# Sums in nine of sixteen steps, lent sums banks and LayerNorm rows on VectorE in a six-layer encoder

## Chip, cores and metric

The kernel runs on one core of a Trainium2 chip. The metric is the device time of one execution in microseconds; the median of three runs of the kernel before is 3676.25 us (3672.96 to 3681.62).

## The reference

Four blocks work on x of shape [2, 1024, 128] in float32, each as `x = x + block(layernorm(x))`: a Mamba block, a mixture of eight experts with the two best chosen, a six-layer attention encoder, and a feed-forward block with weights and activations rounded to a four-bit format. The change lies in the encoder. One encoder layer, with 16 heads of 8 elements, 1024 positions and two batches, computes:

```
q, k = h @ Wq.T + bq, h @ Wk.T + bk            # per head: [1024, 8]
A    = sum over heads of softmax(q k' / sqrt(8))
A    = softmax((A + 16 exp(-|i - j| / 16)) / 16)   # a second softmax, over the mean of the heads
h1   = LN2(LN1(h + A @ h))                      # each LN with its own gain and shift
f    = relu(h1 @ W1.T + b1) @ W2.T + b2         # 512 hidden units
h    = LN3(h1 + f)
```

This is read from the kernel as well as from the reference: the kernel sums the heads' probabilities before the second exponential. q and k are split into three bfloat16 parts each, so that the score products run in bfloat16.

## The kernel before, in words

The four blocks run one after another (`mamba`, `moe`, `encoder`, `fp4_ffn`). In the class `Encoder` the order of all instructions on PE, DVE, ACT and POOL is the program's own, written out by hand in `run`; only the queue SP, which issues most DMAs, is ordered by the framework.

The encoder has 6 layers x 2 batches = 12 attentions, which alternate between the batches. One attention is 8 tiles of 128 queries, one tile is 16 steps, one per head, so there are 1536 steps. In step s:

- `scores` (L986) issues four score products into a tile `sc` of 128x1024 float32 (L1003), then DVE's negated row maximum (L1010). `sc` has three buffers (`pss`, L692), taken in turn with tag "sc".
- `exponentials` of step s-2 (L1013) lets ACT write `e`, 128x1024, with the row sums z. Every fourth time `scaled` (L1025) takes the reciprocals of z on DVE and multiplies four `e` by them on POOL (L1033).
- The sums over heads (`added`, L1060; `offset` for the distance term, L1052) lag by 8 steps and more. Each is 16 transposing products of PE (L1042) that add into two half-size PSUM tiles, `acc0` and `acc1` (128x512 each, `psa`, L693), which I call the sums banks. The table SUMS (L668) says which heads are added in which of the 16 lagged steps: from step 2 to 15.
- After the last head `second` (L1065) takes the second exponential of the sums on ACT (L1070, `prT`); `mixed` (L1075) multiplies it with h on PE (L1080, `sa`: eight products of 128x129), and `residual` (L1089) divides and adds h on DVE (L1094, L1095).

With p = s mod 16, the sums of a tile stand at p = 10 to 15 and 0 to 7, `second` at p = 7, `mixed` at 9, `residual` at 10.

Between two attentions of a batch comes `between` (L923), once for each half of the batch (four tiles): LN1, LN2, a transposition (`transposed`, L772), four products with W1 ("f1", L942), the products with W2 for four row tiles ("f2", L957), LN3, and `project` (L834): a transposition, the products for q and k ("bq", "bk", L853), their three bfloat16 parts on POOL (L870), stores of these to DRAM, and loads of the next q and k (`load_queries`, L895; `load_keys`, L907). q tiles have three buffers, k tiles five, `e` tiles twelve. A norm (L784) takes statistics on DVE, a logarithm and an exponential on ACT, seven small operations on POOL, four row operations on ACT (L818), and gain and shift on POOL (L828, L830).

These pieces are generators. One piece (in every fourth step two) is advanced per step by `advance_one` (L1137); a yielded number makes a piece wait so many steps, and HOLD marks a product whose result is copied out in the next step by `release`. Every product of these pieces, and `sa`, takes one of the three score buffers through `psum` (L730).

Of the kernel before, what the change touches and what calls it, by code (L numbers as in the profile page):

```python
# [18 lines left out]
P = 128  # L19
# [597 lines left out]

def load_encoder(c, wp, w):

    nc = c.nc  # L620
    t = {}
    for k, n in (("b1", NL * FF // P), ("bq", NL), ("bk", NL)):
        t[k] = wp.tile([n, P], F32, name=f"e_{k}n")
        nc.gpsimd.dma_start(t[k], w[k].rearrange("l (c p) -> (l c) p", p=P))
    return t
# [7 lines left out]
HOLD = "hold"  # L633


class Encoder:
# [30 lines left out]

    SUMS = [  # L668
        (), (), (0,), (1,), (2,), (3,), (4,), (5, 6), (7,), (8,), (9,), (10,), (11, 12), (13,),
        (14,), (15,),  # L670
    ]
    QS = (slice(0, P // 2), slice(P // 2, P))
    BEHIND = 2
    TH = TB // 2
    HL = L // 2

    def __init__(self, c, ctx, x, w, t):
        self.c, self.nc, self.tc = c, c.nc, c.tc
        self.x, self.w, self.t = x, w, t
        nc, tc = self.nc, self.tc  # L680
        pool = lambda name, bufs, **kw: ctx.enter_context(tc.tile_pool(name=name, bufs=bufs, **kw))
        self.wp = pool("c_w", 1)
        self.wl = pool("c_wl", 2)
        self.small = pool("c_small", 3)
        self.act = pool("c_act", 2)
        self.parts = pool("c_parts", 1)
        self.ep = pool("c_e", 12)
        self.kp = pool("c_k", 5)
        self.qp = pool("c_q", 3)
        self.loop = pool("c_loop", 2)  # L690
        self.dram = pool("c_dram", 2, space=bass.MemoryType.DRAM)
        self.pss = pool("c_pss", 3, space=PSUM)  # L692
        self.psa = pool("c_psa", 1, space=PSUM)  # L693
        self.scale = float(DH) ** -0.5
        wp = self.wp

        nrel = 2 * L - P
        self.rel = wp.tile([P, nrel], F32, name="rel")
        nc.gpsimd.iota(
            self.rel,  # L700
            pattern=[[-1, nrel]],
            base=L - P,
            channel_multiplier=1,
            allow_small_or_imprecise_dtypes=True,
        )
        nc.scalar.activation(self.rel, self.rel, AF.Abs, bias=c.zero)
        nc.scalar.activation(self.rel, self.rel, AF.Exp, bias=c.zero, scale=-1.0 / DECAY)
        nc.gpsimd.tensor_scalar(self.rel, self.rel, float(NH), 0.0, ALU.mult, ALU.add)

        self.cols = {}  # L710
        for k in ("b1", "bq", "bk"):
            n = t[k].shape[0]
            src = t[k]
            if k != "b1":
                src = wp.tile([n, DH, NH], F32, name=f"e_{k}o")
                nc.gpsimd.tensor_copy(src, t[k].rearrange("l (h d) -> l d h", d=DH))
                src = src.rearrange("l d h -> l (d h)")
            ps = self.psum(f"ps_e_{k}")
            nc.tensor.transpose(ps[:, :n], src, c.ident[:n, :n])
            self.cols[k] = wp.tile([P, n], F32, name=f"e_{k}")  # L720
            nc.scalar.mul(self.cols[k], ps[:, :n], self.scale if k == "bq" else 1.0)
        self.eps = wp.tile([P, 1], F32, name="eps")
        nc.gpsimd.memset(self.eps, EPS)
        self.weights = {}
        self.h = [None] * B
        self.hn = [None] * B
        self.r = [None] * B
        self.qk = [None] * B

    def psum(self, name):  # L730
        return self.pss.tile([P, L], F32, tag="sc", name=name)

    def layer(self, l):
# [14 lines left out]
        yield 8  # L748
        for k, r in raw.items():
            n = r.shape[1]  # L750
            t[k] = wl.tile([P, n * P], F32, tag=f"{k}T", name=f"{k}T_{l}")
            ps = self.psum(f"ps_{k}_{l}")
            for i in range(n):
                nc.tensor.transpose(ps[:, i * P : (i + 1) * P], r[:, i, :], self.c.ident)
            yield HOLD
            if k == "wqk":
                nc.scalar.copy(
                    t[k].rearrange("p (i d h) -> p i h d", i=n, d=DH),
                    ps[:, : n * P].rearrange("p (i h d) -> p i h d", i=n, d=DH),
                )  # L760
            else:
                nc.scalar.copy(t[k], ps[:, : n * P])
            yield
# [8 lines left out]
    def transposed(self, src, who):  # L772
        n = src.shape[1]
        ps = self.psum(f"tp_{who}")
# [3 lines left out]
        dst = self.act.tile([P, n * P], F32, tag="hT", name=f"hT_{who}")  # L778
        self.nc.scalar.copy(dst, ps[:, : n * P])  # L779
        yield  # L780
        yield 1
        return dst

    def norm(self, dst, src, who, gain=None, shift=None):  # L784
# [12 lines left out]
        yield 3  # L797
# [6 lines left out]
        yield 1  # L804
# [7 lines left out]
        nc.gpsimd.tensor_mul(v, mv[:, :, 0], r)  # L812
        nc.gpsimd.tensor_scalar(v, v, -1.0, 0.0, ALU.mult, ALU.add)
        yield
        yield 5
        for q in range(0, n, 2):
            for t in range(q, q + 2):
                nc.scalar.activation(  # L818
                    dst[:, t, :],
                    src[:, t, :],  # L820
                    AF.Identity,
                    bias=v[:, t : t + 1],
                    scale=r[:, t : t + 1],
                )
            yield
        if gain is not None:
            shape = [P, n, D]
            nc.gpsimd.tensor_mul(dst, dst, gain.unsqueeze(1).to_broadcast(shape))  # L828
            yield
            nc.gpsimd.tensor_add(dst, dst, shift.unsqueeze(1).to_broadcast(shape))  # L830
            yield
            yield 4

    def project(self, l, b, half):  # L834
# [8 lines left out]
        if half == 0:  # L843
# [4 lines left out]
            self.qk[b] = {"who": f"{l}_{b}", "q": dq, "k": dk, "kt": [], "qt": []}  # L848
        qk = self.qk[b]
        hT = yield from self.transposed(self.hn[b][:, th * half : th * half + th, :D], f"h_{who}")  # L850
        for i, k in enumerate(("bq", "bk")):
            ps = self.psum(f"ps_{k}_{who}")
# [35 lines left out]
        if half == 1:  # L888
            self.load_queries(b)
# [33 lines left out]
    def between(self, l, b, half):  # L923
# [9 lines left out]
        yield from self.norm(r, r, f"c1_{who}", tl["ln1_w"], tl["ln1_b"])  # L933
        yield from self.norm(r, r, f"c2_{who}", tl["ln2_w"], tl["ln2_b"])
        h2T = yield from self.transposed(r, f"h2_{who}")

        h2b = act.tile([P, th, D], F32, tag="h2b", bufs=1, name=f"h2b_{who}")
        nc.gpsimd.tensor_add(h2b, r, tl["b2"].unsqueeze(1).to_broadcast([P, th, D]))
        ff = act.tile([P, NF, hl], F32, tag="ff", bufs=1, name=f"ff_{who}")
        for k in range(NF):  # L940
            ps = self.psum(f"ps_f1_{who}_{k}")
# [12 lines left out]
        for m in range(th):  # L954
            ps = self.psum(f"ps_f2_{who}_{m}")
            for k in range(NF):
                nc.tensor.matmul(  # L957
                    ps[:, :P],
                    ff[:, k, m * P : (m + 1) * P],
                    tl["w2"][:, k * P : (k + 1) * P],  # L960
                    start=k == 0,
                    stop=k == NF - 1,
                )
            yield HOLD
            nc.vector.tensor_add(r[:, m, :], ps[:, :P], h2b[:, m, :])
            yield
        if half == 0:
            self.hn[b] = self.hidden(b, f"{l}_{b}")
        hn = self.hn[b][:, hs, :D]
        yield from self.norm(hn, r, f"c3_{who}", tl["ln3_w"], tl["ln3_b"])  # L970
        if l + 1 < NL:
            yield from self.project(l + 1, b, half)
        else:
            at = b * TB + half * th
            nc.gpsimd.tensor_add(self.x[:, at : at + th, :], hn, self.x[:, at : at + th, :])

    def begin(self, i):
# [5 lines left out]
        self.h[b] = self.hn[b]  # L983
        return {"l": l, "b": b, "who": who, "h": self.h[b], "r": r, "qk": self.qk[b]}

    def scores(self, a, s):  # L986
# [4 lines left out]
        if hh == 0:  # L991
            for k in ("nm", "z"):
                a[k, m] = self.small.tile([P, NH], F32, tag=k, name=f"{k}_{a['who']}_{m}")
            if m + 2 < TB:
                self.load_queries(a["b"])
        if m == 0 and hh % self.GH == 0 and hh // self.GH + 2 < NH // self.GH:
            self.load_keys(a["b"])
# [67 lines left out]
    def second(self, a, m):  # L1065


        t = self.loop.tile([P, TB, P], F32, tag="prT", name=f"prT_{a['who']}_{m}")
# [6 lines left out]
    def mixed(self, a, m):  # L1075

        prT = a.pop(("prT", m))
        sa = self.psum(f"sa_{a['who']}_{m}")
# [20 lines left out]
    def run(self):  # L1099
# [16 lines left out]
        def add(b, pieces):  # L1116
            work.append([b, pieces, None, 0])

        def advance(i, now):
# [9 lines left out]
            return not wait  # L1129
# [6 lines left out]

        def advance_one(now):  # L1137

            more = 1 + (now % 4 == 3)
            for entry in list(work):  # L1140
                if entry[3] <= now and entry in work:
# [16 lines left out]
        for s in range(n + lag + 2 * NH):  # L1158
            if got := tile_at(s, NH + 3):
                a, m = got  # L1160
                if m % th == th - 1:
                    add(a["b"], self.between(a["l"], a["b"], m // th))
            if s < n:
                if s % steps == 0:
                    i = s // steps
                    while any(entry[0] == i % B for entry in work):
                        advance(0, s)
                    atts[i] = self.begin(i)
                    if i % B == B - 1 and i // B + 1 < NL:
                        work.insert(0, [None, self.layer(i // B + 1), None, 0])  # L1170
                self.scores(*of(s))
            if got := tile_at(s, NH + 2):
                self.residual(*got)
            if 0 <= s - lag < n:
                first = s - lag - (s - lag) % NH
                for hh in self.SUMS[(s - lag) % NH]:
                    a, t = of(first + hh)
                    if hh == 0:
                        self.offset(a, t // NH)
                    self.added(a, t)  # L1180
# [5 lines left out]
            release(s)  # L1186
            if got := tile_at(s, NH - 1):
                self.second(*got)
            if got := tile_at(s, NH + 1):
                self.mixed(*got)  # L1190
            else:
                advance_one(s)
        while work:
            advance(0, s)
# [195 lines left out]
```

## Time and profile before

| what | value |
|---|---|
| median of the runs | 3676.25 us (3672.96 to 3681.62) |
| profiled execution, its own time | 3673.36 us |
| its span | 3671.6 us |
| mean granted TensorE clock | 0.858 |
| from the first to the last score reduce | 676.7 to 3441.9 us |
| busy over the span | PE 79%, DVE 68%, ACT 68%, POOL 69% |
| POOL scaling of `e`, L1033 | 1536 x 1120 ns |
| sums, L1042 | 24576 products, 1043.0 us |
| second exponential, L1070 | 192 x 685 ns |

In a row of the groups stand line, engine, operation, what is written and read with shapes, the count, then busy time in us and the mean ns of one, then the engine's idle time just before these instructions and who ended most of it. In the timeline each row has its start and length in us, and in brackets the idle time before it with its releaser. PEld is the loading of weights, which overlaps PE.

### The profile page before, as it was taken

The numbers are of one execution on the slowest core, as the hardware profiler recorded it, in microseconds if no ns is written. First come the engines' busy times: TensorE is split into PE (matmuls) and PEld (weight loads), VectorE is DVE, ScalarE is ACT, GpSimd is POOL, SyncE is SP. The second block draws the span as 40 slices with busy tenths as digits, with TensorE's granted clock in tenths as the row PEclk, the third lists the DMA queues.
The fourth block names the chain that finished last, engine by engine and source line by source line (L and its number), as shares of the span: only waits on it lengthen the run. The fifth ranks groups of instructions, "written<-read, shape, count | busy, mean of one in ns | idle before, by whom it ended". The sixth has DMA issues, their size and how long they took to land. (4 is left out here: it accounts for less than half of the span.)

```text
span 3671.6 us, 90632 instructions
## 1 busy us (share of the span) xinstructions
PE 2900.8 (79%) x37447; PEld 2099.1 (57%) x37447; DVE 2504.6 (68%) x4058; ACT 2478.4 (68%) x4506; POOL 2522.8 (69%) x2792
## 2 busy tenths in 40 slices
PE   5656996588888888888888888888888888888735
PEld 2345664366666666666666666666666666666513
DVE  6887443376777676667677677676777767777487
ACT  4553344477877777778777787777777777778532
POOL 3996002666877887878778787777877788787632
PEclk8656998688899888889899888998899988999856
DMA  2443001611212221122212222122211221120000
GB/s 79 117 133 83 1 1 30 157 28 40 57 28 64 58 71 35 43 69 60 70 29 50 69 54 65 38 53 69 53 47 47 51 74 51 38 52 21 2 7 11
DMA packets 206163, 193.35 MB, mean 53 GB/s; under 512 B 127700, under 2 KB 170533, under 8 KB 202293
## 3 DMA queue, kind: packets, MB, share of 16 engines
q1 hardware_dynamic: 204884, 184.90, 19.8%
q8 instruction: 293, 4.80, 0.5%
q0 software_dynamic: 864, 2.66, 0.2%
q14 instruction: 122, 0.99, 0.1%
HBM read 129.56 MB, written 57.93 MB: 51 GB/s over the span
## 5 line engine op out<-in xcount | busy, mean ns | idle before, releaser
L1010 DVE TENSOR_REDUCE nm<-sc 128x1 f32<-128x1024 f32 x1536 | 1829.4, 1216 | 853.5 <-PE sc L1003 848.5
L1033 POOL TENSOR_SCALAR e<-e,rz 128x1024 f32<-128x1024 f32 x1536 | 1690.1, 1120 | 559.1 <-DVE rz L1030 487.7
L1016 ACT ACTIVATE e<-sc,nm 128x1024 f32<-128x1024 f32 x1536 | 1704.0, 1115 | 472.7 <-DVE rz L1094 209.6
L1003 PE MATMUL sc<-k,q 36*128 36x512 bf16 x6144 | 1024.7, 406 | 363.3 <-ACT e L1016 282.0
L1042 PEld LDWEIGHTS acc<-ident,e 64*128 64x128 f32 x24576 | 1038.5, 143 | 283.8 <-POOL e L1033 64.1
L1042 PE MATMUL acc<-ident,e 64*128 64x64 f32 x24576 | 1043.0, 227 | 36.2 <-POOL e L1033 33.6
L1003 PEld LDWEIGHTS <-q 36*128 36x128 bf16 x6144 | 284.5, 98 | 601.8 <-issue 528.9
L1016 ACT ACTIVATION_READ_ACCUMULATOR e<-sc,nm 128x1 f32 x1536 | 307.1, 200 | 0.0
L1080 PEld LDWEIGHTS sa<-h,prT 128*128 128x128 f32 x1280 | 253.1, 303 | 73.3 <-ACT e L1016 67.9
L1080 PE MATMUL sa<-h,prT 128*128 128x129 f32 x1280 | 273.6, 399 | 20.3 <-ACT e L1016 18.6
L286 PE MATMUL ys<-ident,yc 128*128 128x128 f32 x512 | 115.0, 388 | 103.5 <-POOL yc L418 86.1
L581 ACT ACTIVATE hT<-ph,b 128x512 f32<-128x512 f32 x128 | 88.0, 687 | 135.6 <-PE ph L574 133.2
L615 POOL TENSOR_TENSOR x<-fo,x 128x512 f32<-128x512 f32 x4 | 5.1, 1280 | 234.7 <-DVE fo L94 234.7
L286 PEld LDWEIGHTS ys<-ident,yc 128*128 128x128 f32 x512 | 86.4, 199 | 138.9 <-POOL yc L418 103.5
L598 DVE SCALAR_TENSOR_TENSOR eo<-po,hot,eo 128x128 f32<-128x128 f32 x256 | 72.0, 344 | 131.7 <-PE po L590 127.4
L369 POOL TENSOR_TENSOR db<-dtx,bb 128x512 f32<-128x512 f32 x128 | 160.9, 1286 | 0.2
L1070 ACT ACTIVATE prT<-acc,zero 128x512 f32<-128x512 f32 x192 | 121.5, 685 | 39.3 <-PE acc L1042 38.1
L590 PEld LDWEIGHTS po<-m_w,hT 128*128 128x128 f32 x1024 | 124.1, 193 | 30.6 <-ACT hT L581 15.7
L356 ACT ACTIVATE da<-dt,zero,na 128x512 f32<-128x512 f32 x128 | 99.7, 781 | 55.0 <-DVE hh L402 51.3
L590 PE MATMUL po<-m_w,hT 128*128 128x128 f32 x1024 | 126.1, 277 | 0.0
L957 PE MATMUL ps_f<-w2T,ff 128*128 128x128 f32 x768 | 109.9, 287 | 7.6 <-ACT e L1016 6.8
L942 PE MATMUL ps_f<-hT_h,w1T 128*128 128x512 f32 x192 | 109.0, 653 | 0.7 <-ACT hT_h L779 0.7
(315 smaller groups left out, 2888.0 us busy)
## 6 DMA issues: line engine op xcount, KB each, us to landing
q<-d_q SPq DMA_DIRECT2D x192, 288.0 KB
bb<-bcd SPq DMA_DIRECT2D x128, 256.0 KB
k<-d_k SPq DMA_DIRECT2D x96, 288.0 KB
d_q<-part_bq SPq DMA_DIRECT2D x192, 128.0 KB
d_k<-part_bk SPq DMA_DIRECT2D x192, 128.0 KB
e_W<-in_L_attn_W SPq DMA_DIRECT2D x12, 256.0 KB
d_q<-part_bq SPq DMA_DIRECT2D x48, 64.0 KB
d_k<-part_bk SPq DMA_DIRECT2D x48, 64.0 KB
```

The lines of the kernel that those rows point to most:

```text
L286: nc.tensor.matmul(ys[k][:, t, :], src[:, t * P : (t + 1) * P], c.ident, is_transpose=True, start=first and t == 0, stop=last, skip_group_ ...
L369: nc.gpsimd.tensor_mul(db[g, k], dtx[b][:, k, halves[h]], bb[g][:, 0, :])
L590: nc.tensor.matmul(po[:, m, :], hT[:, k, m * P : (m + 1) * P], t["w2"][:, e, k, :], start=k == 0, stop=k == NHC - 1,)
L942: nc.tensor.matmul(ps[:, :hl], tl["w1"][:, k * P : (k + 1) * P], h2T, start=True, stop=True)
L957: nc.tensor.matmul(ps[:, :P], ff[:, k, m * P : (m + 1) * P], tl["w2"][:, k * P : (k + 1) * P], start=k == 0, stop=k == NF - 1,)
L1003: nc.tensor.matmul(sc[:, i * self.HL : (i + 1) * self.HL], q[rows, n, hh, :], k[rows, hh % self.GH, n, :], start=n == 0, stop=n == 1,)
L1010: nc.vector.tensor_reduce(a["nm", m][:, hh : hh + 1], sc, AX.X, ALU.max, negate=True)
L1016: self.nc.scalar.activation(e, a.pop(("sc", s)), AF.Exp, bias=a["nm", m][:, hh : hh + 1], accum_out=a["z", m][:, hh : hh + 1],)
L1033: nc.gpsimd.tensor_scalar(e, e, rz[:, i : i + 1], 1.0, ALU.mult, ALU.mult)
L1042: self.nc.tensor.matmul(a["acc", m][k][:, TB - 1 - n, :], src[q, at(n) : at(n) + P], self.c.ident[q, q], is_transpose=True, start=start an ...
L1070: self.nc.scalar.activation(t[:, :, q], a["acc", m][k], AF.Exp, bias=self.c.zero, scale=1.0 / NH)
L1080: self.nc.tensor.matmul(sa[:, : D + 1], prT[:, TB - 1 - n, :], a["h"][:, n, :], start=n == 0, stop=n == TB - 1,)
```

## The change

It does the following; everything outside the encoder stays.

- The sums over heads stand in lagged steps 7 to 15, mostly two heads a step (p = 15 and 0 to 7). `second` stays at p = 7. `mixed` moves to p = 10 and writes into `acc0`; `residual` moves to p = 11.
- At p = 9, 11 and 13 `acc1`, and at p = 12 `acc0`, is lent to one waiting product of the work between attentions. Such a product yields NEED and waits. At even p from 0 to 6, from step 48 of an attention on, a product of the batch whose attention comes next may take a score buffer instead.
- Two f2 row tiles share one buffer, and one addition empties it.
- The row operations of a norm go from ACT to DVE, with the mean and the factor as two operands; two small POOL operations go away. Gain and shift of LN2 and of LN3 are folded into the copy that follows the transposition (per-column operands, `column`); POOL applies them to the untransposed rows after that (`affine`). `ln2_b` is added to `b2` once per layer.
- The half at the end of an attention goes to the head of the work list; `alone` keeps two halves from being in the same stage.
- `e` has 15 buffers in place of 12, q 2 in place of 3, `prT` 1 in place of 2. The q tile of the next tile of queries is loaded at the start of the present one (before: the one after the next), and the next attention's q and k only when the present attention has issued its own q loads.

```diff
-HOLD = "hold"
+HOLD, NEED = "hold", "need"
...
     SUMS = [
-        (), (), (0,), (1,), (2,), (3,), (4,), (5, 6), (7,), (8,), (9,), (10,), (11, 12), (13,),
-        (14,), (15,),
+        (), (), (), (), (), (), (), (0,), (1, 2), (3, 4), (5, 6), (7, 8), (9, 10), (11, 12), (13,),
+        (14, 15),
     ]
+    LENT = {1: 1, 3: 1, 4: 0, 5: 1}
+    LATE = 48
...
+    TO_ACT, FROM_POOL = 3, 5
...
-        self.ep = pool("c_e", 12)
+        self.ep = pool("c_e", 15)
...
-        self.qp = pool("c_q", 3)
+        self.qp = pool("c_q", 2)
...
     def psum(self, name):
+        if self.lent is not None:
+            return self.psa.tile([P, 512], F32, tag=f"acc{self.lent}", name=name)
         return self.pss.tile([P, L], F32, tag="sc", name=name)
...
+    def alone(self, what):
+
+        while what in self.busy:
+            yield 1
+        self.busy.add(what)
+
+    def column(self, k, l):
+        i = LN_COLS.index(k) * NL + l
+        return self.cols["ln"][:, i : i + 1]
+
+    def affine(self, dst, src, gain, shift):
+
+        shape = [P, src.shape[1], D]
+        self.nc.gpsimd.tensor_mul(dst, src, gain.unsqueeze(1).to_broadcast(shape))
         yield
-        yield 1
-        return dst
-
-    def norm(self, dst, src, who, gain=None, shift=None):
+        self.nc.gpsimd.tensor_add(dst, dst, shift.unsqueeze(1).to_broadcast(shape))
+        yield
+
+    def norm(self, dst, src, who):
...
-        nc.gpsimd.tensor_mul(v, mv[:, :, 0], r)
-        nc.gpsimd.tensor_scalar(v, v, -1.0, 0.0, ALU.mult, ALU.add)
...
-                nc.scalar.activation(
+                nc.vector.tensor_scalar(
                     dst[:, t, :],
                     src[:, t, :],
-                    AF.Identity,
-                    bias=v[:, t : t + 1],
-                    scale=r[:, t : t + 1],
+                    mv[:, t, 0:1],
+                    r[:, t : t + 1],
+                    ALU.subtract,
+                    ALU.mult,
                 )
...
+        self.busy.discard("project")
+        qk["halves"] += 1
+        if qk["halves"] == 2:
+            while self.loads:
+                yield 1
             self.load_queries(b)
             self.load_keys(b)
             self.load_keys(b)
...
-        yield from self.norm(r, r, f"c1_{who}", tl["ln1_w"], tl["ln1_b"])
-        yield from self.norm(r, r, f"c2_{who}", tl["ln2_w"], tl["ln2_b"])
-        h2T = yield from self.transposed(r, f"h2_{who}")
+        yield from self.norm(r, r, f"c1_{who}")
+        yield from self.affine(r, r, tl["ln1_w"], tl["ln1_b"])
+        yield self.FROM_POOL
+        yield from self.norm(r, r, f"c2_{who}")
+        yield from self.alone("ffn")
+        h2T = yield from self.transposed(
+            r, "h2", who, self.column("ln2_w", l), self.column("ln2_b", l)
+        )
...
-            if m + 2 < TB:
+            if m + 1 < TB:
                 self.load_queries(a["b"])
+                self.loads -= 1
...
-        t = self.loop.tile([P, TB, P], F32, tag="prT", name=f"prT_{a['who']}_{m}")
+        t = self.loop.tile([P, TB, P], F32, tag="prT", bufs=1, name=f"prT_{a['who']}_{m}")
...
-        sa = self.psum(f"sa_{a['who']}_{m}")
+        sa = self.psa.tile([P, D + 1], F32, tag="acc0", name=f"sa_{a['who']}_{m}")
...
+        def lend(now, bank):
+
+
+            late = now % steps >= self.LATE
+            for i, entry in enumerate(work):
+                if entry[2] is NEED and (
+                    bank is not None or late and entry[0] == (now // steps + 1) % B
+                ):
+                    self.lent = bank
+                    advance(i, now)
+                    self.lent = None
+                    return
...
             release(s)
+            step = (s - lag) % NH
+            if got := tile_at(s, NH + 2):
+                self.mixed(*got)
+            if step in self.LENT:
+                lend(s, self.LENT[step])
+            elif step >= 8 and step % 2 == 0:
+                lend(s, None)
+            if 0 <= s - lag < n:
+                for hh in self.SUMS[step]:
+                    a, t = of(s - lag - step + hh)
+                    if hh == 0:
+                        self.offset(a, t // NH)
+                    self.added(a, t)
             if got := tile_at(s, NH - 1):
                 self.second(*got)
-            if got := tile_at(s, NH + 1):
-                self.mixed(*got)
-            else:
-                advance_one(s)
+            advance_one(s)
```

## The prediction

> **What bounds the kernel now.** I read the page's costliest groups first, then the encoder stretch by windows, the waits, and the timeline of one tile of queries.
>
> ```profile
> L1010 DVE TENSOR_REDUCE nm<-sc 128x1 f32<-128x1024 f32 x1536 | 1829.4, 1216 | 853.5 <-PE sc L1003 848.5
> L1016 ACT ACTIVATE e<-sc,nm 128x1024 f32<-128x1024 f32 x1536 | 1704.0, 1115 | 472.7 <-DVE rz L1094 209.6
> L1003 PE MATMUL sc<-k,q 36*128 36x512 bf16 x6144 | 1024.7, 406 | 363.3 <-ACT e L1016 282.0
> ```
>
> ```profile
> 676.00:3442.00 2766.00, 2337.40 (x34811) 1726.65 (x34810) 1961.48 (x2741) 2123.44 (x3857) 2145.72 (x2396) 0.89 0.21 52
> ```
>
> The second answer's columns are PE, PEld, DVE, ACT, POOL, clock, DMA share, GB/s. No engine is full over the encoder (PE 85%, POOL 78%, ACT 77%, DVE 71%): a loop of three waits for itself. DVE waits for scores, PE for an exponential that frees one of three score buffers, ACT for DVE. The reduces start from 676.7 to 3441.9 us, so a tile of 16 steps takes 2765.2 / 96 = 28.8 us. Folded by p = step mod 16 (mean of the reduce starts, layers 1 to 5), a step takes 1.13 us where nothing interferes, but 2.4 at p=8 and 4.4 at p=9:
>
> ```profile
> 2015.07 0.67 PE L1042 MATMUL acc<-ident,e 64*128 64x64 f32 x16
> 2015.57 0.61 PE L1003 MATMUL sc<-k,q 36*128 36x512 bf16 x4
> 2015.77 1.27 ACT L1070 ACTIVATE prT<-acc,zero 128x512 f32<-128x512 f32 x2 [1.34 <-PE acc L1042]
> 2016.92 1.11 ACT L1016 ACTIVATE e<-sc,nm 128x1024 f32<-128x1024 f32 x1
> 2018.18 0.82 PE L1003 MATMUL sc<-k,q 36*128 36x512 bf16 x4 [2.00 <-ACT e L1016]
> 2019.28 3.28 PE L1080 MATMUL sa<-h,prT 128*128 128x129 f32 x16 [0.28 <-ACT e L1016]
> 2022.49 0.61 PE L1003 MATMUL sc<-k,q 36*128 36x512 bf16 x4
> 2024.45 1.11 ACT L1016 ACTIVATE e<-sc,nm 128x1024 f32<-128x1024 f32 x1 [2.90 <-DVE rz L1094]
> ```
>
> The second softmax (L1070) waits for the last sums and delays an exponential; PE waits 2.0; then `sa` (L1080) takes a score buffer and 3.28 us of PE, and ACT runs dry. The granted clock has mean 0.61 in that interval, 0.94 or more in most others. This is the first cost that the change attacks; the second is between-attention work in the same ring. PE's own price per step, full clock:
>
> ```profile
> 2001.32 0.61 PE L1003 MATMUL sc<-k,q 36*128 36x512 bf16 x4 [0.51 <-ACT e L1016]
> 2001.75 1.17 PE L1042 MATMUL acc<-ident,e 64*128 64x64 f32 x32
> 2002.74 0.61 PE L1003 MATMUL sc<-k,q 36*128 36x512 bf16 x4
> 2003.18 0.67 PE L1042 MATMUL acc<-ident,e 64*128 64x64 f32 x16
> 2003.68 0.61 PE L1003 MATMUL sc<-k,q 36*128 36x512 bf16 x4
> ```
>
> Start to start, 1.42 us with two heads of sums, 0.94 with one (medians over the trace 1.42 and 0.95; at half clock 2.51 and 1.71). An f1 product adds 1.14, an f2 row tile 1.24, bq or bk 1.34, a transposition 0.67.
>
> **Spine of a tile, before and after.** I walk the loop without between-work. Before: p=8 2.4, p=9 4.4, p=10 1.7, thirteen steps at 1.13, and 0.3 more at each of the two two-head steps: 23.8 us.
>
> After, the sums stand at p=15 and 0 to 7. From p=15 to p=7 PE is the bound: one step with head 0 and the offset (1.42), six with two heads (8.5), one with a single head (0.95) = 10.9 us against 1.13 per reduce, so DVE and ACT have slack there. From p=7 to the next p=15, times from the scores at p=7 (T): its two heads end at T+1.4, the softmax at 2.7, the delayed exponential at 3.8, so scores of p=9 at 3.9 (before: the same wait, one head shorter). Scores of p=10 wait for the next exponential, 4.95. Then `sa`, now in a sums bank, 3.4 us: the mean of L1080 (271.7 us for 79 tiles), since the same idle precedes it as now. Scores at 8.8, 9.25, 9.7; the first reduce at 9.45, exponentials to 11.85 and 12.95, so p=15 at 13.1. Spine: 13.1 + 10.9 = 24.0. Lending a bank to `sa` alone therefore buys nothing: what leaves p=9 comes back as PE-bound steps. With `sa` at full clock (2.1 us, a gapless step) it is 22.7.
>
> **Between-work.** Before it costs 28.8 - 23.8 = 5.0 us a tile, 0.4 of it DMA waits (below); 24 buffers per attention and 1.5 for the weights make 3.2 a tile. Counting the new loop by hand, an attention issues about 12 uses in lent banks (1.5 a tile) and about 9 in the score ring, late, at even p from 0 to 6.
> - Ring uses: 2 f2 pairs, 4 f1, 2 or so of bq/bk, a transposition: 12.9 us of PE per attention, 1.6 a tile, in full because PE is the bound there.
> - Lent uses: PE has 5.1 us of idle between T and the next p=15 to hold them (13.1 less eight score groups at 0.45, two heads at 0.49, `sa` 3.4). One before `sa` delays by 0 to 0.6, one after it by 0.5, their evictions fall where ACT is dry: 0.5 a tile.
> - No ring use remains for `sa`, which is in the spine already.
>
> **LayerNorm rows.** 72 norms x 4 = 288 activations of 490 to 500 ns leave ACT: 141 us of busy time. DVE gets 288 tensor_scalar. The same instruction is L80:
>
> ```profile
> 3526.95 1.06 POOL L1233 TENSOR_TENSOR a_u<-a_u,am_u 128x512 f32<-128x512 f32 x1 [5.79 <-DVE r_d L72]
> 3527.00 1.09 DVE L80 TENSOR_SCALAR u<-x,mv_d,r_d 128x128 f32<-128x128 f32 x1
> ```
>
> Its median is 0.34 us; three of sixteen took 1.08 to 1.09, each beside a POOL operation whose end it waited for. The Trainium skill ("SBUF — State Buffer", Who interferes with whom) says why and speaks against this change: a VectorE tensor_scalar that uses both port pairs and a GpSimd instruction exclude each other, the first to issue keeping the pair for its whole length. By the median a pair of rows costs 0.68 us; by the rule, with POOL busy 78% of the encoder, 0.78 x 2.2 + 0.22 x 0.68 = 1.9 us. I take 1.9: 1.5 pairs a tile, 2.8 us of DVE. Not all is path: a reduce delayed by 1.8 us reaches PE three scores later, where a PE-bound stretch has 1.3 in hand (0.5 left), and `sa` leaves DVE 2.3 us idle. About 0.7 a pair, 1.0 a tile. Bounds: 0 and 2.8. Behind a row stands the next reduce, for it ACT, then PE. The ACT pairs that go (0.98 each, in a stretch with ACT at 1.09 of 1.13) are in the 5.0.
>
> **Edits at nothing.** POOL loses two small operations per norm (0.39) and one net 128x512 operation per half (1.27), about 58 us; it has slack and its `e` is used six steps later. The transposition's copy becomes an activation with bias (0.59 to 0.69, as L858), +0.1 in 44. Adding `ln2_b` to `b2` and the new column transposes are once-only. `e` at 15 buffers: exp for the seventeenth step follows head 0's sum by two steps; no wait. One `prT`: thirteen steps lie between its reader and next writer. In the tail (3442 to 3500) nine heads of sums become fifteen (+3) and the norm chain loses about 5: nothing.
>
> **Queues.** Loads of q move to one tile ahead with two buffers. Each waits on SP until the tile before has ended, then takes about 5 us of DMA (2001.96 to 2006) under a 27 us tile; behind it on SP stand part stores and k loads. Cost zero; if that cover went, about 4.4 a tile, as now in attention 0, whose loads for the other batch take q buffers: eight waits on `q<-d_q`, 17 us. Those go, since the new loads wait for the attention's own. The four waits of 4.4 to 5.3 us on `k<-d_k` at attention starts (19 us) should go too: the project work ends at step 111 of 128 by my count, where the trace shows the k loads issued at step 122. Together 0.4 a tile, not carried over. If k still waits, 19 us return.
>
> **Sum.** 24.0 + 1.6 + 0.5 + 1.0 = 27.1 us a tile; (28.8 - 27.1) x 96 = 163. The profiled execution took 3673.4 (span 3671.6), so 3510; the median of the runs is 2.9 higher, which I leave inside the rounding. **3510 us.**
>
> **Rivals.**
> *Better (0.24):* `sa` stays at full clock because lent products fill the idle before it (-1.3), and the rows hide (-0.7): 25.1 a tile would be 3318; half of this is likelier, 26.1, about 3415. For: PE has work at p=9 and 11 to 13. Against: the 2 us wait at p=8 is unchanged.
> *Slower by the port (0.12):* the row pairs are fully exposed, 2.8 instead of 1.0 a tile: +173, 3683. It decides from about 2.7 us exposed a tile. For: the 1.09 rows, and POOL issuing four scalings back to back. Against: the slack in the PE-bound stretch.
> *Slower by the clock (0.10):* the sums, now dense transposes, run at half clock: 1.09 us for each of seven two-head steps, 7.6 a tile. From 22% of such steps the gain is gone; at a third, 2.5 a tile, 3750. The Trainium skill ("TensorE: Matmul & The Clock Gate", Part 4) says that transpose-mode work does not bring the full clock. By the rule the dense stretch could be cold; but of 105 gapless two-head steps in the trace 95 ran wholly at full clock, so I follow the row: the score products among them suffice.
> *As summed (0.54):* 3440 to 3590.
>
> The chances: faster 0.78 (as summed and better), slower 0.18, and 0.04 within 0.2% (about 7 us, what a measurement of this kernel can tell from no change) from the edge of the port case. The range 3385 to 3690 leaves out the strongest gains (0.07) and most of the cold case (0.09).
>
> **What would show it.** By p, intervals near 1.4 at p=0 to 6, not 1.13; p=9 down from 4.4; a new wait of about 3 us just after `sa`, at p=10; row operations at 0.34 and 1.1 mixed; PE's wait for ACT's `e` less than 282; no q or k waits after attention 0. Wrong would be: two-head steps well over 1.5, a wait on `q<-d_q` in each tile, or the waits for rows and reduces growing on DVE.

## The result and the profile after

The kernel after takes 3777.04 us (median of 4 runs, 3765.58 to 3779.48) against 3674.61 us (3668.82 to 3681.62) for the kernel before on the same chip: ratio 1.0272, 95% interval 1.0243 to 1.03. It is 2.7% slower where I forecast 4.5% faster. The profiled execution took 3779.1 us, its span is 3777.4 us, and its mean granted clock is 0.820 (before: 0.858). In these traces the granted clock is 1.00 or 0.50 at any moment, so a value between them is a mixture over time; I call the time at 0.50 half clock.

From the costliest groups of the kernel after, the same loop and the two kinds of new waiting:

```profile
L1075 DVE TENSOR_REDUCE nm<-sc 128x1 f32<-128x1024 f32 x1536 | 1849.3, 1218 | 541.9 <-PE sc L1068 525.9
L1081 ACT ACTIVATE e<-sc,nm 128x1024 f32<-128x1024 f32 x1536 | 1702.1, 1114 | 447.4 <-DVE nm L1075 282.8
L1068 PE MATMUL sc<-k,q 36*128 36x512 bf16 x6144 | 1052.4, 426 | 453.5 <-ACT e L1081 419.8
L1001 ACT ACTIVATE ff<-ps_f,e_b 128x512 f32<-128x512 f32 x96 | 66.1, 689 | 187.1 <-PE ps_f L997 187.1
```

DVE waits less for scores (853.5 before, 541.9 now), but PE waits more for an exponential (282 before, 420 now), and ACT now stands 187 us before the copy of an f1 product, since a copy is next in ACT's hand-written order and PE has not made the product yet. The encoder by windows (stretch, length, busy us of PE, PEld, DVE, ACT and POOL, granted clock, DMA share, GB/s):

```profile
676.00:3557.00 2881.00, 2419.03 (x34712) 1701.38 (x34713) 2171.46 (x2966) 2038.35 (x3584) 2095.77 (x2244) 0.84 0.19 50
```

PE issues nearly the same number of products (34811 before), yet is busy 82 us longer: its clock fell from 0.89 to 0.84. The stretch is 115 us longer; the wait of attention 0 for q and the waits for k that I had expected to go are gone, and attention 0 took 213.7 us instead of 234.2. In attentions 1 to 10, counted from 0, a tile takes 30.5 us against 28.9.

Where the clock is lost shows in one tile, cut by its stages and read by windows: dense sums; wait and one f1 product; `sa`; single score groups and a second f1 product; first sums; next dense stretch.

```profile
2127.40:2136.90 9.50, 9.50 (x244) 8.30 (x242) 8.03 (x9) 7.37 (x13) 8.84 (x13) 1.00 0.05 12
2136.90:2142.10 5.20, 3.20 (x21) 0.72 (x16) 4.96 (x8) 5.04 (x10) 3.23 (x4) 0.89 0.00 0
2142.10:2145.20 3.10, 3.10 (x20) 2.98 (x20) 1.75 (x2) 2.39 (x5) 3.10 (x4) 0.64 0.00 0
2145.20:2151.10 5.90, 4.08 (x39) 1.69 (x40) 5.42 (x8) 3.82 (x7) 4.85 (x5) 1.00 0.11 21
2151.10:2154.50 3.40, 3.40 (x60) 2.96 (x57) 2.24 (x2) 2.46 (x7) 2.77 (x3) 0.51 0.64 173
2154.50:2160.00 5.50, 5.50 (x142) 4.79 (x140) 4.80 (x13) 3.91 (x7) 3.32 (x4) 0.99 0.04 9
```

PE is full in the first stretch and has clock 1.00. Then it works 3.20 us of 5.20, and `sa` runs at 0.64; then 4.08 of 5.90, and the sums start at 0.51. In this tile the loss comes behind each thin stretch, and hits what comes next; the fold over all tiles below shows the same places. The second is new. PE's rows there, from the timeline:

```profile
2151.96 1.08 PE L1068 MATMUL sc<-k,q 36*128 36x512 bf16 x4
2152.81 1.92 PE L1107 MATMUL acc<-ident,e 64*128 64x64 f32 x32
2154.52 0.65 PE L1068 MATMUL sc<-k,q 36*128 36x512 bf16 x4
2154.99 1.16 PE L1107 MATMUL acc<-ident,e 64*128 64x64 f32 x32
2155.98 0.39 PE L1068 MATMUL sc<-k,q 36*128 36x512 bf16 x2
```

The same work, four score products and two heads of sums, takes 2.56 us start to start and then 1.46. Folded by p over attentions 1 to 10, the clock in the intervals p = 9, 10, 13, 14, 15 and 0 is 0.65, 0.68, 0.86, 0.74, 0.61 and 0.75, and 0.99 from p = 1 to 6. Before, it was 0.61 at p = 9, 0.84 at p = 8, and 0.94 or more elsewhere. A tile spends 9.4 us at half clock, before 5.9. PE's busy share in the same fold is 0.31 at p = 8 and 0.35 and 0.65 at p = 12 and 13; before, p = 8 had 0.40 and p = 10 to 15 all 0.83 or more.

### The profile page after: what moved, and what is told of

It reads as the page before. It is cut to its first block, busy times and chain, and to the rows that moved or that the text cites. A ratio compares the mean times of both kernels' runs of the same rounds, so it can differ in the third digit from the quotient of the medians.

```text
span 3777.4 us, 90640 instructions
## 1 busy us (share of the span) xinstructions
PE 2987.9 (79%) x37448; PEld 2078.8 (55%) x37448; DVE 2726.7 (72%) x4314; ACT 2382.4 (63%) x4203; POOL 2469.5 (65%) x2626
## 5 line engine op out<-in xcount | busy, mean ns | idle before, releaser
L1075 DVE TENSOR_REDUCE nm<-sc 128x1 f32<-128x1024 f32 x1536 | 1849.3, 1218 | 541.9 <-PE sc L1068 525.9
L1068 PE MATMUL sc<-k,q 36*128 36x512 bf16 x6144 | 1052.4, 426 | 453.5 <-ACT e L1081 419.8
L1107 PEld LDWEIGHTS acc<-ident,e 64*128 64x128 f32 x24576 | 979.6, 150 | 219.0 <-issue 60.5
L1107 PE MATMUL acc<-ident,e 64*128 64x64 f32 x24576 | 997.6, 234 | 12.1 <-POOL e L1098 11.6
L1145 PEld LDWEIGHTS sa<-h,prT 128*128 128x128 f32 x1280 | 234.5, 282 | 55.8 <-issue 55.8
L1145 PE MATMUL sa<-h,prT 128*128 128x129 f32 x1280 | 253.0, 376 | 0.0
L1001 ACT ACTIVATE ff<-ps_f,e_b 128x512 f32<-128x512 f32 x96 | 66.1, 689 | 187.1 <-PE ps_f L997 187.1
L858 DVE TENSOR_SCALAR r<-r,mv_c,r_c 128x128 f32<-128x128 f32 x192 | 141.6, 780 | 3.9 <-POOL r_c L853 2.1
L590 PEld LDWEIGHTS po<-m_w,hT 128*128 128x128 f32 x1024 | 125.1, 195 | 30.5 <-ACT hT L581 15.7
L1159 DVE RECIPROCAL rz<-sa 128x1 f32<-128x1 f32 x96 | 16.2, 169 | 166.1 <-PE sa L1145 166.1
L997 PE MATMUL ps_f<-h2T,w1T 128*128 128x512 f32 x192 | 131.7, 778 | 3.2 <-ACT prT L1135 1.4
```

Source lines behind the costliest of these rows:

```text
L590: nc.tensor.matmul(po[:, m, :], hT[:, k, m * P : (m + 1) * P], t["w2"][:, e, k, :], start=k == 0, stop=k == NHC - 1,)
L858: nc.vector.tensor_scalar(dst[:, t, :], src[:, t, :], mv[:, t, 0:1], r[:, t : t + 1], ALU.subtract, ALU.mult,)
L997: nc.tensor.matmul(ps[:, :hl], tl["w1"][:, k * P : (k + 1) * P], h2T, start=True, stop=True)
L1068: nc.tensor.matmul(sc[:, i * self.HL : (i + 1) * self.HL], q[rows, n, hh, :], k[rows, hh % self.GH, n, :], start=n == 0, stop=n == 1,)
L1075: nc.vector.tensor_reduce(a["nm", m][:, hh : hh + 1], sc, AX.X, ALU.max, negate=True)
L1107: self.nc.tensor.matmul(a["acc", m][k][:, TB - 1 - n, :], src[q, at(n) : at(n) + P], self.c.ident[q, q], is_transpose=True, start=start an ...
```

## The experiments

My theory after the result: **the clock.** Gathering the sums in nine steps leaves PE thin from p = 8 to 14, so the clock halves there and stays halved into the first sums. Rivals: **the port** (rows on DVE), and **the order of ACT's work**, where copies of lent products stand ahead of exponentials and wait.

The ratios are each to the kernel before on the same chip; its median lies between 3670.03 and 3682.28 us from chip to chip, so a difference of some 12 us between kernels below is not told from none.

### The port

**after, with the row operations back on ACT.** The two small POOL operations come back with them; the same edit is used further down.

```diff
-                nc.vector.tensor_scalar(
-                    dst[:, t, :], src[:, t, :], mv[:, t, 0:1], r[:, t : t + 1],
-                    ALU.subtract, ALU.mult,
+                nc.scalar.activation(
+                    dst[:, t, :], src[:, t, :], AF.Identity,
+                    bias=v[:, t : t + 1], scale=r[:, t : t + 1],
```

> The kernel after with one part undone: the row operations of the encoder's norms are back on ACT, with the two small POOL operations that they need. Three theories for the 100 us lost. Clock: gathering the sums leaves PE a light stretch of seven steps in which the granted clock falls (half-clock time up from 5.9 to 9.4 us a tile), at a price of about 1.7 us a tile. Queue: lent and late products stand on PE behind sa or two-head sums, and their copies stand on ACT ahead of the next exponential (ACT's idle before ff went from 46 to 187 us). Port: the rows on DVE, 0.78 us each in place of 0.34, hold up the reduces. By the port theory this kernel takes 3680 or less. By the clock and the queue theories it stays between 3740 and 3800, since 288 x 0.49 us return to ACT, which has 9 us idle a tile.

Measured: 3776.67 us, ratio to before 1.0276 (1.0258 to 1.0294), the time of the kernel after. The rows' place makes no difference there.

**before, with the row operations on DVE and nothing else** (the reverse edit, without the two small POOL operations).

> The kernel before with one part of the change alone: the norms' row operations on DVE, two small POOL operations fewer. By the port theory this alone costs most of the 100 us: 3750 or more. By the clock and the queue theories it costs nothing or gains a little, because ACT gives up 141 us in a stretch where ACT and DVE are both near their bound: 3640 to 3690.

Measured: 3762.17 us, 1.0277 (1.0219 to 1.0335): alone, the rows cost 90 us, 2.8%. The instructions of the row line, first this kernel's (L816), then the kernel after's (L858), with min, median and max in ns:

```profile
L816 DVE TENSOR_SCALAR r<-r,mv_c,r_c x192: 310/350/1337, 835.3 to 3562.0; 128x128 f32<-128x128 f32 x192
L816 DVE TENSOR_SCALAR h<-r,mv_c,r_c x96: 318/1138/1400, 954.0 to 3582.8; 128x128 f32<-128x128 f32 x96
```

```profile
L858 DVE TENSOR_SCALAR r<-r,mv_c,r_c x192: 309/982/1270, 817.1 to 3582.9; 128x128 f32<-128x128 f32 x192
L858 DVE TENSOR_SCALAR h<-r,mv_c,r_c x96: 315/366/1336, 1003.1 to 3600.9; 128x128 f32<-128x128 f32 x96
```

Both show the mixture that I named, about 0.34 and 1.1 us, and nearly the same mean over the 288 (0.77 and 0.74). The slow rows wait for POOL: in the kernel after, 157 of the 288 took over 0.6 us, and 145 of these began while a POOL instruction ran and ended within 0.1 us of its end. The operation is as slow in both kernels, and costs 90 us in one and nothing in the other. The traces of attentions 1 to 10 show what the rows, some 2.3 us of DVE a tile, displace. With gathered sums they fill idle time of DVE (9.3 us a tile with rows on ACT, 7.6 on DVE), and the tile grows by 0.1 us only; in the kernel before they fill less of it (8.4 and 7.4), and the tile grows by 0.9. The rows also stand elsewhere: in the kernel before 1.4 of the 2.3 us lie at p = 0 to 3, in the kernel after 0.6. Part of the 90 us is clock as well, since half clock rises from 5.9 to 7.4 us a tile. How the 90 us divide among these is not separated.

### The two halves of the change

**after, with the table of sums, the place and buffer of `sa`, and the issue of the between-work as before.** Folded gains, paired f2 rows, buffers, loads, order of the halves and rows on DVE stay.

```diff
-        (), (), (), (), (), (), (), (0,), (1, 2), (3, 4), (5, 6), (7, 8), (9, 10), (11, 12), (13,),
-        (14, 15),
+        (), (), (0,), (1,), (2,), (3,), (4,), (5, 6), (7,), (8,), (9,), (10,), (11, 12), (13,),
+        (14,), (15,),
...
-        sa = self.psa.tile([P, D + 1], F32, tag="acc0", name=f"sa_{a['who']}_{m}")
+        sa = self.psum(f"sa_{a['who']}_{m}")
...
-            if step in self.LENT:
-                lend(s, self.LENT[step])
-            elif step >= 8 and step % 2 == 0:
-                lend(s, None)
```

> The kernel after with the sums back in lagged steps 2 to 15, sa and all work between attentions in the score ring again, sa and its residual in their old steps; rows on DVE, the folded gains, the paired f2, the buffers and the loads stay as after. By the clock theory half-clock time falls to about 6 us a tile and the time to 3640 to 3700. By the queue theory the same, with ACT's idle before ff back under 80 us. By the port theory it stays above 3740.

Measured: 3689.35 us, 1.0043 (1.0028 to 1.0058), with 6.3 us of half clock a tile. Gathering and lending together cost 88 us.

**The same with the rows on ACT.**

> The kernel after with the sums, sa and the work between attentions as before (the wide run, 3689) and also the rows on ACT; what is left of the change is the folded gains of LN2 and LN3, the paired f2, the order of the halves, the buffers and the loads. If the 90 us that rows on DVE cost the kernel before are in the wide run too, this takes 3590 to 3620, and the rest of the change is worth 60 us or more. If not, 3670 to 3700.

Measured: 3632.73 us, 0.9867 (0.9846 to 0.9889), between the two ranges that I had given. So the rest of the change is a gain of 42 us by the medians; with wide sums the rows cost 57. The account of the 102 us by medians: rest -42, rows +57, gathering and lending +88. With the rows on ACT, gathering and lending cost 144 (3776.67 less 3632.73): the two costs do not add up, so either hides part of the other.

### The clock

These kernels add work: one product of 128x512 float32 per named step, into a sums bank whose content is done with. Nothing reads it. If PE's work were what is missing, this makes a kernel slower; if the clock is, it makes it faster.

**after, with the unread product in lagged steps 0 and 6 (p = 8 and 14), 192 in all.**

```diff
+    WARM = {0: 0, 6: 0}
...
+        ps = self.psa.tile([P, 512], F32, tag=f"acc{bank}", name=f"warm_{s}")
+        self.nc.tensor.matmul(ps, self.c.ident, self.rel[:, :512], start=True, stop=True)
```

> The kernel after with work added: in lagged steps 0 and 6 of each tile PE makes one more product of 128x512 in float32 (as large as an f1, 1.1 us at full clock) into acc0, which nothing reads. By the clock theory PE's idle time there is filled, half-clock time falls from 9.4 to 7 us a tile or less, and the time falls by 30 us or more although 192 products are added. By the queue and the port theories the products only cost: 3790 to 3900.

Measured: 3636.6 us, 0.9896 (0.9878 to 0.9915): 140 us less than the kernel after, with more work. Half clock falls from 9.4 to 4.5 us a tile.

**The same with a third, in lagged step 5 (p = 13), 288 in all.**

> The kernel after with three products a tile that nothing reads, in lagged steps 0, 5 and 6 (288; the run with steps 0 and 6 took 3637). That run kept a clock of 0.81, 0.70 and 0.74 at p = 13, 14 and 15. By the clock theory a product at p = 13 removes this second dip: clock above 0.9 there, half-clock time under 3.5 us a tile, 3570 to 3630. If the rest of the loss is in the queues, the added product costs what it takes: 3640 to 3720.

Measured: 3604.11 us, 0.9798 (0.9778 to 0.9819); 2.5 us of half clock, `sa` 2.10 us in the mean (3.20 in the kernel after). The encoder by windows:

```profile
676.00:3390.00 2714.00, 2446.09 (x35470) 1570.50 (x35467) 2159.45 (x2967) 2039.95 (x3586) 2106.25 (x2248) 0.96 0.20 53
```

An unread product takes 1.12 us of PE at full clock, so 288 are at least 323 us; PE's busy time rose by 27 only (2419 to 2446). So at least 296 us of PE's busy time in the kernel after are gone, by this estimate the price of the same work at a slower clock. The unread products are ordinary ones; whether transposing products would hold the clock as well, no run shows.

**before, with one unread product, at p = 8, 96 in all.**

> The kernel before with one product of 128x512 that nothing reads added at p = 8 of each tile (96 in all) into acc0, where PE waits about 2 us for an exponential. The last runs speak for the clock: 192 such products took 140 us off the kernel after and its half-clock time from 9.4 to 4.5 us a tile. By the clock theory the kernel before, with 5.9 us of half clock a tile of which most lies at p = 8 and 9, gains too: its clock at p = 9 rises from 0.61 to 0.9 or more, and the time falls by 40 to 110 us, to 3560 to 3630. If the light stretch of the kernel after was special and the products help in another way there, 96 products of 1.1 us cost 0 to 100 us here: 3670 to 3770.

Measured: 3572.08 us, 0.9706 (0.9684 to 0.9728). The kernel before had the same loss in one place, and it was worth 103 us, as much as the change lost. Windows of the encoder, then the timeline about p = 8 and 9 of this kernel:

```profile
676.00:3340.00 2664.00, 2315.45 (x35073) 1636.58 (x35074) 1960.43 (x2742) 2125.76 (x3863) 2155.36 (x2400) 0.95 0.22 54
```

```profile
2021.49 1.27 ACT L1070 ACTIVATE prT<-acc,zero 128x512 f32<-128x512 f32 x2
2021.51 0.61 PE L1003 MATMUL sc<-k,q 36*128 36x512 bf16 x4
...
2022.23 1.12 PE L1091 MATMUL warm<-rel,ident 128*128 128x512 f32 x2
...
2025.00 0.61 PE L1003 MATMUL sc<-k,q 36*128 36x512 bf16 x4 [0.38 <-ACT e L1016]
...
2025.54 2.05 PE L1080 MATMUL sa<-h,prT 128*128 128x129 f32 x16
```

PE does at least 107 us more products and is busy 22 us less than before (2315 against 2337). The product (L1091) lies where PE waited 2.0 us, and `sa` takes 2.05 us instead of 3.28.

**after, rows on ACT, two unread products; then three.**

> The kernel after with the two products a tile in lagged steps 0 and 6 (3637 with the rows on DVE) and the row operations back on ACT. In the kernel after the rows' place made no difference (3777 on ACT, 3777 on DVE), in the kernel before DVE cost 90 us. If the cold clock hid the rows, because PE was late anyway, they show once it is gone: 3560 to 3610. If it is the denser sums that leave DVE room, nothing changes: 3620 to 3660.

> The gathered sums and loans with three unread products (3604 with the rows on DVE), rows on ACT. With the rows on ACT and sums, sa and between-work in their old places one unread product gave 3531. If the clock is all that gathering and lending cost, this takes 3530 to 3560. If they cost through queues and new waits as well, 3600 to 3640, about what it takes with the rows on DVE.

Measured: 3662.76 us, 0.9954 (0.9928 to 0.998), and 3595.63 us, 0.98 (0.9767 to 0.9833). Against the versions with rows on DVE that is 26 more and 8 less: in none of the three pairs with gathered sums do rows on DVE cost time that these runs can tell. Why they were 26 us better there with two products is open.

**Wide sums with one unread product at p = 8: rows on ACT, then on DVE.**

> The wide run with the rows on ACT (3633) and the one unread product a tile at p = 8 that took 103 us off the kernel before. Its clock at p = 9 was 0.61. If the two gains are independent (folded gains, order of the halves and loads on the one side, clock on the other), it takes 3530 to 3560. If the rest of the change gained only by shortening the wait in which the clock falls, it stays at 3570 to 3600.

> The wide run (sums, sa and the work between attentions as before, rows on DVE; 3689) with the one unread product a tile at p = 8. Against the gathered sums and loans with unread products (3604) it says what gathering and lending cost when the clock is held up in both; without the products they cost 88 us (3777 against 3689). If nearly all of that is the clock, this takes 3580 to 3610. If 40 us or more of it are queues and new waits, it takes 3565 or less. If the products help the wide run less than the 102 us that they gave on ACT, more than 3620.

Measured: 3530.88 us, 0.9597 (0.9572 to 0.9622), and 3622.13 us, 0.9847 (0.9804 to 0.9891). The first is the fastest of all, 4.0% below the kernel before. The rows cost 91 us between them, with 2.5 and 3.6 us of half clock a tile.

### The order of ACT's work, the bank, and the loans

**after with three unread products, copies of products lent at p = 9 and 11 issued two steps later.**

```diff
+            work[i][4] = now + 1 + (self.lent is not None and (now - lag) % NH < 4)
...
-                if entry[2] is HOLD:
+                if entry[2] is HOLD and entry[4] <= now:
```

> The run with three unread products a tile (3604), with the copies of products lent at p = 9 and 11 issued two steps later instead of one. ACT still idles 1.1 us a tile before ff there, and its p = 11 product stands on PE behind sa. By the queue theory the later copy frees the exponential in front: ACT's idle before ff falls below 0.6 us a tile and the time to 3560 to 3590. If these waits cost nothing, or move to the bank's next user, 3600 to 3630.

Measured: 3596.63 us, 0.9774 (0.9751 to 0.9797), 7 us less. ACT's waits over the encoder, first with the copies where the change has them, then with the later copies (us in total, times, longest):

```profile
ACT e L1082 <- DVE nm L1076: 211.8, 336, 3.5
...
ACT ff L1002 <- PE ps_f L998: 94.3, 81, 3.4
```

```profile
ACT e L1082 <- DVE nm L1076: 420.7, 438, 26.4
```

```profile
ACT ff L1002 <- PE ps_f L998: 7.8, 6, 2.9
```

The copies' wait falls from 94 to 8 us (this last row is from a window 30 us longer), and ACT waits 209 us more for maxima instead. ACT was early at these places; the wait is where its slack shows, not a cost. So this rival falls with the clock held; in the kernel after itself, where the wait is 187 us, the later copies were not tried.

**before with one unread product, `sa` in `acc0` one step later, sums moved back to make room.**

```diff
-        (), (), (0,), (1,), (2,), (3,), (4,), (5, 6), (7,), (8,), (9,), (10,), (11, 12), (13,),
-        (14,), (15,),
+        (), (), (), (), (0,), (1,), (2, 3), (4,), (5, 6), (7,), (8,), (9, 10), (11,), (12, 13),
+        (14,), (15,),
...
-        sa = self.psum(f"sa_{a['who']}_{m}")
+        sa = self.psa.tile([P, D + 1], F32, tag="acc0", name=f"sa_{a['who']}_{m}")
```

> The kernel before with its unread product (3572), and of the change only the loan to sa: sa goes to acc0 at p = 10, its residual to p = 11, and the sums are moved to lagged steps 4 to 15 (four two-head steps instead of two). My walk says that p = 9 falls from 3.4 to about 1.2 us, p = 10 rises from 1.8 to about 3, and the two more two-head steps cost up to 0.6: a gain of 0.4 us a tile or more, 3510 to 3545. If the loan only moves the cost, as the walk said of the whole change, 3565 to 3600.

Measured: 3647.52 us, 0.9905 (0.9874 to 0.9937): 75 us slower than with `sa` in a score buffer and the sums in their old steps. PE's waits in it show a new one:

```profile
PE sc L1003 <- ACT e L1016: 169.5, 311, 1.4
PE acc L1042 <- DVE r L1099: 121.1, 91, 1.4
```

The distance term, the next writer of `acc0`, waits for the residual on DVE to read `sa`; p = 12 takes 2.59 us (1.43 with a score buffer), at clock 0.81. I had not seen this wait. It is this kernel's own: in the change the first sum comes at p = 15, and no such wait appears.

**Gathered sums, rows on ACT, three unread products, no loans to the between-work:** its products take score buffers at once, `sa` stays in `acc0`.

```diff
-            return not wait and got is not NEED
+            return not wait
...
-            if step in self.LENT:
-                lend(s, self.LENT[step])
-            elif step >= 8 and step % 2 == 0:
-                lend(s, None)
```

> The same with the loans to the work between attentions undone: its products take a score buffer in the step in which they come up, as before; the sums stay gathered, sa stays in acc0. If it is the copies of lent products, standing on ACT before the next exponential, that cost, this is faster than the run with the loans by 25 us or more. If it is the gathering itself (PE idle early in the tile, then late), it is the same or slower, since products then take score buffers again in stretches where PE is full.

Measured: 3601.73 us, 0.9827 (0.9787 to 0.9867), against 3595.63 with the loans: no difference that these runs can tell. With the clock held and the rows on ACT, lending the banks to the between-work neither gains nor costs.

## Why the prediction was wrong, point by point

**The step that failed is the spine after.** It charged `sa` "3.4 us: the mean of L1080 ..., since the same idle precedes it as now", and every other product its full-clock price. That confines the half clock to `sa`, and puts a cold start of the first sums at nothing. But taking the sums out of p = 10 to 14 is what thins PE there. Mean intervals of attentions 1 to 10 in us, against my terms, and with three unread products a tile for comparison:

| part of a tile | term | after | three unread products |
|---|---|---|---|
| p = 15 and 0, first sums | 2.8 | 4.5 | 3.4 |
| p = 1 to 6, dense sums, with ring uses | 8.1 + 1.6 | 10.0 | 10.5 |
| p = 7 to 14, with lent uses | 13.1 + 0.5 | 16.0 | 14.8 |
| rows | 1.0 | 0 | 0 |
| tile | 27.1 | 30.5 | 28.7 |

- **p = 15 and 0:** +1.7, at clock 0.61 and 0.75. This is the cold start that the sum left out.
- **p = 1 to 6:** right within 0.3. Two-head steps run at full clock once PE has been full: of 421 that PE did without a gap at p = 1 to 5, 377 ran wholly at full clock and none wholly at half; of 62 such steps at p = 0, 14 ran wholly at full clock and 31 wholly at half.
- **p = 7 to 14:** +2.4. The wait after `sa` came as forecast (p = 10 3.5 us, new), and p = 9 fell from 4.4, but to 2.0 at clock 0.65 where I had walked 1.05 and up to 0.6 for a lent product. p = 11 to 14 took 1.5 to 1.6 us a step where I walked 1.1. The clock explains part only: with three unread products they still took 1.5 to 1.9, two of the products among them. DVE is the busiest engine there (90% of 6.2 us, 4.8 of it the four reduces and 0.6 the rows), and the same four steps took 5.7 us in the kernel before, work between attentions included. With the rows on ACT they took 5.8 instead of 6.2, but the tile as a whole 30.3. What else holds these steps is open.
- **Rows:** the wait for POOL is real, and rows on DVE cost 90 us in before, but the term of 1.0 a tile is 0 here. A pair took 1.5 us in the mean where I took 1.9. I had said that there is slack in the PE-bound stretch; most of the rows went into idle time of DVE (9.3 to 7.6 us a tile).
- **PE's wait for `e`** rose to 420 where I expected less than 282. Most of the rise stands before the scores of p = 13 to 15 (2.0 us a tile, before 0.4), in the stretch that the sums have left, and the wait before p = 9 stays (2.1, before 1.6).
- **Queues:** right. Outside the start of the encoder no wait for q or k of note is left.

**The rivals.** The one by the clock had the right engine and cause, at 0.10, but the wrong place: the dense sums, by the rule on transposes. That rule is not what happened; those steps, score products among them, show 0.99. That its figure of 3750 lies near the measured 3777 is luck. Another place in the same page bears on it. The Trainium skill ("TensorE: Matmul & The Clock Gate", A second HAM failure mode) tells of another kernel in which short idle times of PE between groups of products, if frequent, let the clock swing between half and full; the page's table under Why this matters for your kernels asks only for no idle times of over about 3 us. By that row alone no half clock was to be expected here: no wait of PE on another engine in the encoder exceeded 2.7 us in the kernel after. The clock fell to 0.51 all the same, so frequent short waits with thin work suffice. The longest row of PE's waits (us in total, times, longest):

```profile
PE ps_bq L896 <- ACT e L1081: 13.4, 5, 2.7
```

The row that should have warned me was my own: 0.61 at p = 9, behind a wait of 2.0 us.

**The missing gain.** Clock alone does not turn the change into a gain. The fair comparison gives both kernels unread products: on one chip, the kernel before then takes 3572.08 us and the kernel after 3604.11, both with 2.5 us of half clock a tile. So of the 102 us lost, some 70 go with the clock, and 32 stay. 3604.11 is also 94 us above my forecast: even at a clock better than I had reckoned with, the gain did not come. With unread products in both, gathering and lending are worth -18 us with rows on DVE (3604.11 against 3622.13, half clock 2.5 and 3.6 us a tile; their intervals overlap) and +65 with rows on ACT (3595.63 against 3530.88, half clock 1.8 and 2.5). I had forecast -163 for the whole. In all three comparisons the gathered version carries two unread products more a tile, 192 x 1.12 = 215 us of PE, and how much of that lies in its idle time was not separated. So that the clock makes most of the loss is shown; what makes the other 32 us, and whether gathered sums could win at full clock without the extra products, stays open.

## What to carry to other kernels

When a change moves PE work together, look at the stretch that it empties: price what follows that stretch at the slow clock, and not only the product that was slow before. Look for a low granted clock behind a thin stretch, and try an unread product there before restructuring: here 96 of them took 2.9% off the kernel before, more than the rest of the change without gathering did (1.3%). And compare two schedules only after both have had that remedy. The same slow operation cost 90 us in one schedule and nothing in another, so its price has to be measured in the schedule in which it will stand.

## What the hardware showed

- Adding PE work shortened every version tried: 96 products of 128x512 float32 took off 103 us (before), 102 and 67 (wide sums, rows on ACT and on DVE), 192 took off 140 and 288 took off 173 (after).
- PE work of 3.2 us in 5.2, or 4.1 in 5.9, was followed by half clock in one tile of the kernel after; no single wait was over 2.7 us. In the mean over attentions 1 to 10, busy shares of PE of 0.31 at p = 8 and 0.35 at p = 12 stood ahead of clocks of 0.65 (p = 9) and 0.61 (p = 15); with three unread products the shares were 0.68 and 0.72, and no interval had a clock under 0.91.
- Row operations of 128x128 on DVE took 0.31 to 1.40 us, in the mean 0.77 (before with rows on DVE) and 0.74 (after), with POOL busy 74% and 73% of the encoder; 145 of the 157 slow ones in the kernel after ended within 0.1 us of the POOL instruction that ran when they began.
